# Attention over cached and new keys: the new keys' probabilities turned with the cached ones, their products one step later

## The chip, the cores and the metric

The kernel runs on one core of one Trainium2 chip. The metric is the device time of one execution in microseconds (us), the median over the runs shown. A core has five engines with a queue of instructions each, which they work off in order: TensorE (PE in the profile; PEld is its loading of weights, which overlaps the matmuls), VectorE (DVE), ScalarE (ACT), GpSimd (POOL) and SyncE (SP), which here only issues DMAs. The engines wait for one another by semaphores.

## The reference

`x` is 32 sequences of 32 tokens with 512 features. Four layers each add their result to `x`:

```python
x = x + einsum('bct,bcd->bdt', x, weights[cond])            # a 32x32 mix of tokens, picked per sequence
x = x + x @ W.T + 0.5 * (x @ lora_A[label]) @ lora_B.T      # picked per sequence
x = x + einsum('bsi,boi->bso', x, weight[adapter])          # picked per sequence
x = x + attention(x)
```

The attention has 32 query heads and 8 key heads of 128 features (4 query heads share a key head). Queries and keys are normalised and rotated by position. Each sequence sees 512 cached keys from 16 pages of a paged cache, masked beyond its cached length, and then its own 32 new keys:

```python
scores = einsum('bqhd,bkhd->bhqk', q, k_all) * SCALE        # k_all: 512 cached, 32 new
scores = where(valid, scores, -1e30)
probs = softmax(scores)
o = einsum('bhqk,bkhd->bqhd', probs, v_all)                 # v_all: 512 cached, 32 new
out = einsum('bse,de->bsd', o.reshape(b, s, 4096), Wo)
```

All is fp32.

## The kernel before

The first part (to some 370 us) computes the first three layers and the projections of queries, keys and values; queries, new keys and new values go to DRAM. The change doesn't touch it. The rest, `with tc.manual_schedule(engines=order)` from L1247 on, is the attention. Its order is written out by hand for all five engines: what the loop issues first on an engine runs first there. Waits are put in by the framework, where an instruction needs another's data, buffer or PSUM bank.

The work is cut into units (b, g): sequence b of 32, key head g of 8. A unit has 128 rows: 4 query heads times 32 tokens. One loop step n stands for the unit n = 8 b + g and does, for several units at different stages:

- `scores` (L1012): two matmuls of TensorE give 128x544 scores in `s_ps` (two PSUM banks, one buffer), and one VectorE operation (L1028) scales and masks them into `pr` and takes the row's minimum, `low`. The next step's scores wait until that has read `s_ps`.
- `exponentials` (L1040): ScalarE, in place, with the row's sum in `dens`.
- `flip_kept` (L1144): VectorE transposes finished outputs `os` into `ot`.
- `fill` (to n = 36) or `share`: one piece of another matmul that has no hurry, to fill TensorE: the last of the value projections, later the output projection of an earlier group of four sequences (`finish`, L1174). `SHARE` says how many of its 32 heads each of 32 steps takes, counted from n = 37 (`BEGIN`) on.
- `place` (L1052) for the unit issued four steps before. Four units with g = 0 to 3 or 4 to 7 form a quarter (b, q), and `pr` and `placed` are per quarter, with two buffers each. The products with the values need the probabilities with the keys on the partitions. In its step j of 4 VectorE turns 32x32 blocks of 128x512 elements of the quarter (L1057: `turned`), and four copies of 32x512 move each band of 32 partitions to its place in `placed`: two on ScalarE and two on GpSimd for q = 0, two on ScalarE and two on VectorE for q = 1, with a third on ScalarE in place of one of VectorE's in its last step (sequence 0 has its own split).
- `gather_new`, `flip_new` (L1077, L1082): once a quarter, the probabilities of the new keys, 4 times 32 columns, are gathered by GpSimd into `pq`, turned by TensorE into PSUM (`pn_ps`) and copied by ScalarE into `pn`.
- `values` (L1088) for the unit issued LAG = 8 steps before: four products of `placed` with the cached values, added up in `o_ps`. That is four PSUM banks with one buffer; bank u holds, side by side, the 128 columns of head u of the first quarter and of the second.
- `new_values` (L1110), after the products of g = 3: eight products of `pn` with the new values, four for each quarter.
- `keep` (L1127), after the last products of a quarter: VectorE takes the reciprocal of the sums (`rden`) and scales that quarter's columns of `o_ps` into `os` (L1133).

In each step the loop issues scores, exponentials, `flip_kept`, `fill`, then `gather_new`, `flip_new` and `place`, then `share`, then `values`. Each matmul in the source is two in the profile's counts, for fp32.

Of the kernel before, what the change touches and what calls it, by code (L numbers as in the profile page):

```python
# [12 lines left out]
F32 = mybir.dt.float32  # L13
# [7 lines left out]
P = 128  # L21
B, S, HID = 32, 32, 512
D, HQ, HK = 128, 32, 8
REP = HQ // HK
PAGES, PSIZE, NPP = 64, 32, 16
L = NPP * PSIZE
# [12 lines left out]
QUAD = 4  # L39
AHEAD = 8  # L40
VS_BUFS = 2
LATE = 12
N_LOW = 9


C_BT, C_SEQ, C_TOK, C_LAB, C_COND = 0, 128, 160, 168, 176
# [13 lines left out]
def cond_resid_kernel(  # L60
# [18 lines left out]
    nc = tc.nc  # L79
# [35 lines left out]
    ident = const.tile([P, P], F32, name="ident")  # L115
# [106 lines left out]
    def load_new_keys(b: int):  # L222
        nc.sync.dma_start(out=kts[b][:, NPP, :], in_=k_d[b])
# [672 lines left out]
    tp = turn.enter_context(tc.tile_pool(name="a_t", bufs=1))  # L896
# [99 lines left out]
    ps_p = ctx.enter_context(tc.tile_pool(name="b_p", bufs=1, space=PSUM, side="right"))  # L996
# [5 lines left out]
    tp = ctx.enter_context(tc.tile_pool(name="b_t", bufs=2, side="right"))  # L1002
# [3 lines left out]
    dens, prs, pos = {}, {}, {}  # L1006
    first = L - N_LOW * PSIZE

# [3 lines left out]
    def scores(b: int, g: int):  # L1012
# [5 lines left out]
        q = qt[:, u * REP * S : (u + 1) * REP * S]  # L1018
        nc.tensor.matmul(ps[:, first:L], q, kt4[:, :N_LOW, g, :], start=True, stop=True)  # L1019
        nc.tensor.matmul(  # L1020
            ps[:, L : first + LT], q, kt4[:, N_LOW:, g, :], start=True, stop=True
        )
# [27 lines left out]
    placed = {}  # L1050

    def place(b: int, q: int, j: int):  # L1052
        if j == 0:
            placed[b, q] = tp.tile([P, QUAD, L // P, P], F32, tag="placed", name=f"placed_{b}_{q}")
        pr = prs[b, q][:, :, :L].rearrange("p u (c j s) -> p j u c s", j=P // S, s=S)[:, j]
        part = tp.tile([P, QUAD, L // P, S], F32, tag="turned", name=f"turned_{b}_{q}_{j}")
        nc.vector.transpose(part, pr)  # L1057

        on_pool = q == 0 or b == 0
        if b == 0:  # L1060
            on_act = 1 + q
        else:
            on_act = 3 if q == 1 and j == QUAD - 1 else 2
        for i in range(P // S):
            dst = placed[b, q][j * S : (j + 1) * S, :, :, i * S : (i + 1) * S]
            src = part[i * S : (i + 1) * S]
            dst, src = (a.rearrange("p u c s -> p (u c) s") for a in (dst, src))
            if i < on_act:
                nc.scalar.copy(dst, src)  # L1069
            elif on_pool:  # L1070
                nc.gpsimd.tensor_copy(dst, src)  # L1071
            else:
                nc.vector.tensor_copy(dst, src)  # L1073

    pqs, pns = {}, {}

    def gather_new(b: int, q: int):  # L1077

        pqs[b, q] = tp.tile([P, QUAD, S], F32, tag="pq", name=f"pq_{b}_{q}", bufs=1)
        nc.gpsimd.tensor_copy(pqs[b, q], prs[b, q][:, :, L:])  # L1080

    def flip_new(b: int, q: int):  # L1082
        pnp = ps_p.tile([P, P], F32, tag="p", name=f"pn_ps_{b}_{q}")
        nc.tensor.transpose(pnp, pqs.pop((b, q)).rearrange("p u s -> p (u s)"), ident)  # L1084
        pns[b, q] = tp.tile([P, P], F32, tag="pn", name=f"pn_{b}_{q}")
        nc.scalar.copy(pns[b, q], pnp)

    def values(b: int, g: int):  # L1088

        vt = vts[b]  # L1090
        q, u = divmod(g, QUAD)
        if g == 0:
            pos[b] = ps_o.tile([P, QUAD, L], F32, tag="o", name=f"o_ps_{b}")
        po = pos[b][:, u, q * D : (q + 1) * D]
        pt = placed[b, q][:, u, :, :]
        for c in range(L // P):
            nc.tensor.matmul(  # L1097
                po,
                pt[:, c, :],
                vt[:, c, g * D : (g + 1) * D],  # L1100
                start=(c == 0 and q == 0),
                stop=(c == L // P - 1 and q == 1),
            )
        if u == QUAD - 1:
            if q == 0:
                new_values(b)
            placed.pop((b, q)), prs.pop((b, q))
            keep(b, q)

    def new_values(b: int):  # L1110

        vn = vns[b]
        for q in range(HK // QUAD):
            pn = pns.pop((b, q))
            for i in range(QUAD):
                r = slice(i * S, (i + 1) * S)
                nc.tensor.matmul(  # L1117
                    pos[b][:, i, q * D : (q + 1) * D],
                    pn[r, :],
                    vn[r, q, :],  # L1120
                    start=(q == 1),
                    stop=(q == 0),
                )

    kept = []

    def keep(b: int, q: int):  # L1127

        po = pos[b] if q == 0 else pos.pop(b)
        rden = tp.tile([P, QUAD], F32, tag="rden", name=f"rden_{b}_{q}")  # L1130
        nc.vector.reciprocal(rden, dens.pop((b, q)))  # L1131
        o = tp.tile([P, QUAD * D], F32, tag="os", name=f"os_{b}_{q}")
        nc.vector.tensor_tensor(  # L1133
            o.rearrange("p (u d) -> p u d", d=D),
            po[:, :, q * D : (q + 1) * D],
            rden.unsqueeze(2).to_broadcast([P, QUAD, D]),
            ALU.mult,
        )


        at = BT * HK * (b // BT) + LAG + HK + QUAD - 2 if (b % BT, q) == (0, 1) else 0
        kept.append((b, q, o, at))
# [60 lines left out]
    LAG = 8  # L1203

    SHARE = [1, 1, 2, 1, 1, 1, 1, 1, 2, 1, 1, 1, 1, 1] + [1, 1, 0] + [1] * 7 + [0] + [1] * 7

    LAST = SHARE[:14] + [1, 1, 0, 1, 0, 1, 1, 1, 1, 1, 0, 1, 0] + [1, 1, 1, 2, 2]
    BEGIN = BT * HK + LAG - QUAD + 1  # L1210

    def share(n: int):
        t, i = divmod(n - BEGIN, BT * HK)
        if 0 <= t < NT - 1:
            parts = LAST if t == NT - 2 else SHARE
            done = sum(parts[:i])
# [4 lines left out]
    units = [(b, g) for b in range(B) for g in range(HK)]  # L1221
# [25 lines left out]
    with tc.manual_schedule(engines=order):  # L1247
        for n in range(N + LAG):
            b, g = divmod(n, HK)
            if n == FILLED + 2:  # L1250
                pa.close()
                late = ctx.enter_context(tc.tile_pool(name="b_w", bufs=1))
                places.append(late)
                wos[1] = late.tile([P, LATE, HID], F32, name="wo_1")
            if BEGIN <= n <= N and n % (BT * HK) == 0:

                load_residual((n - BEGIN) // (BT * HK))
            if n < N:
                if g == 0 and b >= 1:
                    load_queries(b, 1)  # L1260
                if g == 0 and 1 <= b < B - 1:
                    load_keys(b + 1)
                    load_new_keys(b + 1)
                    keys.dsts = page_keys(b + 1)
                    keys.transfer(slice(0, 12))
                if g < L // P and b >= 2:
                    load_value_chunk(b, g)
                if g == QUAD and b < B - 1:
                    load_queries(b + 1, 0)
                    load_inverses(b + 1)  # L1270
                    if b >= 1:
                        keys.transfer(slice(12, NPP))
                    if 1 <= b < B - 2:
                        load_table(b + 2)
                if g == QUAD + 1 and b >= 1:
                    load_new_values(b)
                if g == QUAD + 2 and b < B - 2:
                    keys = Picked(nc.sync, k_cache, pages_of.pop(b + 2), range(NPP), K_SHAPE)
                scored = scores(b, g)
                exponentials(*scored)  # L1280
            flip_kept(n)
            fill(n)
            if n in unstored:
                store_values(*unstored.pop(n))
            if n == QUAD + 1:
                load_new_values(0)
            if n in WO_AT:
                load_wo(2 * WO_AT.index(n))
            if QUAD <= n < N + QUAD:
                bq, i = divmod(n - QUAD, HK)  # L1290
                q, j = divmod(i, QUAD)
                if j == 0:
                    gather_new(bq, q)
                if j == 2:
                    flip_new(bq, q)
                place(bq, q, j)
            share(n)
            if n >= LAG:
                values(*units[n - LAG])
            if n < N and g == HK - 1 and b < B - 1:  # L1300
                see_keys(b + 1)
            if n > N + QUAD:
                at = 4 * (n - N - QUAD - 1)
                finish(NT - 1, range(at, at + 4))
        assert not dens and not prs and not pos and not placed and not pns
        load_residual(NT - 1)
        flip_kept(N + LAG)
        finish(NT - 1, range(3 * QUAD, HALF))
        finish_by_halves(NT - 1)
# [76 lines left out]
```

## Time and profile before

| | |
|---|---|
| median of 3 runs (lowest to highest) | 1139.23 us (1138.83 to 1139.81) |
| the profiled execution | 1139.8 us, its span 1138.0 us |
| granted TensorE clock | 1.00 |
| busy: TensorE, VectorE, ScalarE, GpSimd | 99%, 71%, 66%, 49% of the span |
| turns of the new keys' probabilities, TensorE (L1084) | 64, 273 ns each, 17.4 us busy |
| their copies out of PSUM, ScalarE (L1086) | 64, 245 ns each |
| their gathers, GpSimd (L1080) | 64, 290 ns each |
| turns of the others, VectorE (L1057) | 256, 698 ns each |
| copies into `placed`: ScalarE, GpSimd, VectorE | 539 of 617 ns, 268 of 611 ns, 217 of 436 ns |
| scaling into `os`, VectorE (L1133) | 64, 692 ns each |

How to read it: matmuls are pipelined, and their ends are modelled, so a matmul's duration isn't the time by which it holds up the next one; the distance of their starts is. "Idle before" is the time an engine stood still ahead of an instruction, with what released it. A group's line gives its source line, engine, operation, the tiles out<-in, its shape and how often it occurs. In a timeline, like instructions that follow each other are merged into one line (x8: eight of them). The first steps of attention start at 373 us, the last scores at 1089.5 us.

### The profile page before, as it was taken

Reading aid. Unit: us, or ns where it says so; the run is one execution under the profiler, and the core shown is the slowest. Engines: PE = TensorE matmul, PEld = TensorE weight load, DVE = VectorE, ACT = ScalarE, POOL = GpSimd, SP = SyncE. Lnnn points to the kernel's source line nnn. Section 1 sums busy time; section 2 is a strip of 40 time slices with the busy share of each in tenths; the row PEclk is TensorE's granted clock in tenths of the full one; section 3 lists DMA queues with packets and bytes.
Section 4 is the critical chain, followed back from the end, with each engine's and each line's share of the span. In section 5 each row is a group of like instructions: output and inputs, shape, how many; then the busy total and the mean of one; then the engine's idle time right before and its main releaser. Section 6 shows DMA issues by size and latency. Waiting matters only on the chain. (4 is left out here: it accounts for less than half of the span.)

```text
span 1138.0 us, 18994 instructions
## 1 busy us (share of the span) xinstructions
PE 1122.4 (99%) x5432; PEld 730.1 (64%) x5432; DVE 807.5 (71%) x1670; ACT 752.8 (66%) x1900; POOL 559.0 (49%) x719
## 2 busy tenths in 40 slices
PE   8999999999999999999999999999999999999998
PEld 5554444444444577777777777777777777777766
DVE  2510688886977487777778868877877777877851
ACT  1211377576666688777777777877777877777750
POOL 3411689899897544533443344334533443344310
PEclk9999999999999999999999999999999999999999
DMA  8998447688786587888667756765776676766610
GB/s 319 392 419 347 176 133 220 174 234 229 197 232 169 159 272 267 271 308 284 216 217 243 248 190 230 262 229 178 243 251 223 200 239 224 240 202 214 222 29 10
DMA packets 173354, 259.24 MB, mean 228 GB/s; under 512 B 31522, under 2 KB 130466, under 8 KB 168770
## 3 DMA queue, kind: packets, MB, share of 16 engines
q1 hardware_dynamic: 152226, 184.22, 51.0%
q0 software_dynamic: 20016, 71.97, 17.7%
q10 hardware_dynamic: 1008, 1.84, 0.4%
q8 instruction: 44, 0.72, 0.3%
q14 instruction: 60, 0.49, 0.1%
HBM read 228.46 MB, written 37.88 MB: 234 GB/s over the span
## 5 line engine op out<-in xcount | busy, mean ns | idle before, releaser
L1069 ACT COPY placed<-turned 32x512 f32<-32x512 f32 x539 | 332.8, 617 | 31.4 <-DVE turned L1057 24.0
L1097 PEld LDWEIGHTS o_ps<-vt,placed 128*128 128x128 f32 x2048 | 267.0, 191 | 118.5 <-issue 89.4
L1028 DVE CUSTOM_DVE_ANT_0 pr<-s_ps,mask,rq 128x544 f32<-128x544 f32 x256 | 200.6, 784 | 132.5 <-PE s_ps L1020 124.0
L1044 ACT ACTIVATE pr<-pr,low 128x544 f32<-128x544 f32 x256 | 192.2, 751 | 132.7 <-DVE low L1028 130.8
L1071 POOL COPY placed<-turned 32x512 f32<-32x512 f32 x268 | 163.6, 611 | 230.8 <-DVE turned L1057 164.1
L1097 PE MATMUL o_ps<-vt,placed 128*128 128x128 f32 x2048 | 270.4, 275 | 5.6 <-ACT placed L1069 2.8
L1174 PE MATMUL f_ps<-wo,ot 128*128 128x512 f32 x480 | 241.3, 594 | 0.7
L1057 DVE STREAM_TRANSPOSE turned<-pr 128x512 f32<-128x512 f32 x256 | 178.7, 698 | 0.1
L1019 PE MATMUL s_ps<-kt,qt 128*128 128x288 f32 x512 | 174.4, 422 | 1.4 <-DVE low L1028 0.5
L1020 PE MATMUL s_ps<-kt,qt 128*128 128x256 f32 x512 | 152.3, 379 | 0.4 <-issue 0.4
L252 POOL DMA_INDIRECT vt<-in_v_cache_dram,v_idx x128 | 128.0, 1000 | 36.6 <-issue 25.4
L1020 PEld LDWEIGHTS s_ps<-kt,qt 128*128 128x128 f32 x512 | 97.2, 190 | 27.5 <-DMA kt<-in_k_cache_dram 0.8
L434 POOL TENSOR_TENSOR ra<-ra,rs 128x512 f32<-128x512 f32 x80 | 103.9, 1306 | 10.6 <-DVE rs L429 6.4
L1174 PEld LDWEIGHTS f_ps<-wo,ot 128*128 128x128 f32 x480 | 85.8, 190 | 28.6 <-issue 13.9
L1073 DVE COPY placed<-turned 32x512 f32<-32x512 f32 x217 | 94.6, 436 | 5.5
L1080 POOL COPY pq<-pr 128x128 f32<-128x128 f32 x64 | 18.6, 290 | 149.4 <-PE o_ps L1097 94.6
L447 ACT ACTIVATE sq<-x 128x128 f32<-128x128 f32 x256 | 76.4, 302 | 19.3 <-DVE x L405 13.9
L1019 PEld LDWEIGHTS s_ps<-kt,qt 128*128 128x128 f32 x512 | 77.3, 191 | 17.0 <-DVE low L1028 10.6
L544 ACT COPY r<-m 128x512 f32<-128x512 f32 x80 | 46.4, 580 | 52.4 <-PE m L389 51.4
L389 PE MATMUL m<-t_pair,x_sums 128*128 128x512 f32 x160 | 75.3, 593 | 0.6 <-ACT r L544 0.6
L389 PE MATMUL m<-w_pair,x3t 128*128 128x512 f32 x160 | 75.2, 592 | 0.0
L389 PE MATMUL m<-w_pair,x_sums 128*128 128x512 f32 x160 | 72.1, 592 | 0.0
(129 smaller groups left out, 1223.6 us busy)
## 6 DMA issues: line engine op xcount, KB each, us to landing
kt<-in_k_cache_dram SPq DMA_DIRECT2D x512, 128.0 KB
wa<-in_w_adapt_dram SPq DMA_DIRECT2D x32, 1024.0 KB
q_d<-st SPq DMA_DIRECT2D x128, 128.0 KB
qt<-q_d SPq DMA_DIRECT2D x64, 256.0 KB
w_pair<-in_w_qkv_dram SPq DMA_DIRECT2D x20, 512.0 KB
o_d<-in_w_o_dram SPq DMA_DIRECT2D x16, 512.0 KB
wo<-o_d SPq DMA_DIRECT2D x16, 512.0 KB
k_d<-st SPq DMA_DIRECT2D x32, 128.0 KB
```

The costliest lines, as they stand in the source:

```text
L252: nc.gpsimd.indirect_dma_start(out=vts[b][:, c, :], out_offset=None, in_=v_cache, in_offset=bass.IndirectOffsetOnAxis(ap=v_idx[:, at : at ...
L389: nc.tensor.matmul(ps, of[:, k], by[:, k], start=(not more and k == 0), stop=(k == KH - 1), skip_group_check=more,)
L434: nc.gpsimd.tensor_tensor(u.a, u.a, u.s, ALU.add)
L1019: nc.tensor.matmul(ps[:, first:L], q, kt4[:, :N_LOW, g, :], start=True, stop=True)
L1020: nc.tensor.matmul(ps[:, L : first + LT], q, kt4[:, N_LOW:, g, :], start=True, stop=True)
L1028: nc.vector.tensor_tensor_reduce(pr, ps[:, first : first + LT], mask, rqs[b][:, g // QUAD, u : u + 1], 3.0e38, ALU.add, ALU.min, low,)
L1044: nc.scalar.activation(pr, pr, AF.Exp, bias=low, scale=-1.0, accum_out=dens[quad][:, u : u + 1])
L1057: nc.vector.transpose(part, pr)
L1069: nc.scalar.copy(dst, src)
L1071: nc.gpsimd.tensor_copy(dst, src)
L1097: nc.tensor.matmul(po, pt[:, c, :], vt[:, c, g * D : (g + 1) * D], start=(c == 0 and q == 0), stop=(c == L // P - 1 and q == 1),)
L1174: nc.tensor.matmul(pfs[t][:, :HID], ots[t, h // HALF][:, h % HALF, :], wo(h), start=(h == 0), stop=(h == (HQ if t < NT - 1 else HALF) - 1),)
```

## The change

The probabilities of the new keys are no longer gathered, turned by TensorE and copied. `placed` becomes 17 blocks of 128 columns a quarter instead of 4 x 4. In step j of `place` VectorE turns a further 128x32 elements, the new keys' columns of the quarter's unit j, into a 17th block of `turned`; the four copies then move 32x544 elements instead of 32x512, so after step 3 the 17th block holds what `pn` held. `gather_new`, `flip_new` and their tiles go. `new_values` reads the 17th blocks of both quarters. The second quarter's is complete only after its last `place`, so `new_values` moves from the end of `values` of g = 3 to just before `values` of g = 4, one step later; `keep(b, 0)` moves with it. The first output head of each group of four sequences is projected one step later (`SHARE` begins 0, 2, 2 instead of 1, 1, 2).

```diff
+NEW = QUAD * (L // P)
...
     def place(b: int, q: int, j: int):
         if j == 0:
-            placed[b, q] = tp.tile([P, QUAD, L // P, P], F32, tag="placed", name=f"placed_{b}_{q}")
+            placed[b, q] = tp.tile([P, NEW + 1, P], F32, tag="placed", name=f"placed_{b}_{q}")
         pr = prs[b, q][:, :, :L].rearrange("p u (c j s) -> p j u c s", j=P // S, s=S)[:, j]
-        part = tp.tile([P, QUAD, L // P, S], F32, tag="turned", name=f"turned_{b}_{q}_{j}")
-        nc.vector.transpose(part, pr)
+        part = tp.tile([P, NEW + 1, S], F32, tag="turned", name=f"turned_{b}_{q}_{j}")
+        nc.vector.transpose(part[:, :NEW].rearrange("p (u c) s -> p u c s", u=QUAD), pr)
+        nc.vector.transpose(part[:, NEW], prs[b, q][:, j, L:])
...
-            dst = placed[b, q][j * S : (j + 1) * S, :, :, i * S : (i + 1) * S]
+            dst = placed[b, q][j * S : (j + 1) * S, :, i * S : (i + 1) * S]
             src = part[i * S : (i + 1) * S]
-            dst, src = (a.rearrange("p u c s -> p (u c) s") for a in (dst, src))
...
-    def gather_new(b: int, q: int):
-
-        pqs[b, q] = tp.tile([P, QUAD, S], F32, tag="pq", name=f"pq_{b}_{q}", bufs=1)
-        nc.gpsimd.tensor_copy(pqs[b, q], prs[b, q][:, :, L:])
-
-    def flip_new(b: int, q: int):
-        pnp = ps_p.tile([P, P], F32, tag="p", name=f"pn_ps_{b}_{q}")
-        nc.tensor.transpose(pnp, pqs.pop((b, q)).rearrange("p u s -> p (u s)"), ident)
-        pns[b, q] = tp.tile([P, P], F32, tag="pn", name=f"pn_{b}_{q}")
-        nc.scalar.copy(pns[b, q], pnp)
...
-        pt = placed[b, q][:, u, :, :]
+        pt = placed[b, q][:, u * (L // P) : (u + 1) * (L // P), :]
...
-        if u == QUAD - 1:
-            if q == 0:
-                new_values(b)
+        if g == HK - 1:
             placed.pop((b, q)), prs.pop((b, q))
             keep(b, q)
...
-            pn = pns.pop((b, q))
+            pn = placed[b, q][:, NEW, :]
...
+        placed.pop((b, 0)), prs.pop((b, 0))
+        keep(b, 0)
...
-    SHARE = [1, 1, 2, 1, 1, 1, 1, 1, 2, 1, 1, 1, 1, 1] + [1, 1, 0] + [1] * 7 + [0] + [1] * 7
+    SHARE = [0, 2, 2, 1, 1, 1, 1, 1, 2, 1, 1, 1, 1, 1] + [1, 1, 0] + [1] * 7 + [0] + [1] * 7
...
-                if j == 0:
-                    gather_new(bq, q)
-                if j == 2:
-                    flip_new(bq, q)
                 place(bq, q, j)
             share(n)
             if n >= LAG:
+                if units[n - LAG][1] == QUAD:
+                    new_values(units[n - LAG][0])
                 values(*units[n - LAG])
```

More of the change, by code (lines that the diff above doesn't have):

```diff
@@ L1073, in place @@
                 nc.vector.tensor_copy(dst, src)
-    pqs, pns = {}, {}
-    def gather_new(b: int, q: int):
-        pqs[b, q] = tp.tile([P, QUAD, S], F32, tag="pq", name=f"pq_{b}_{q}", bufs=1)
-        nc.gpsimd.tensor_copy(pqs[b, q], prs[b, q][:, :, L:])
-    def flip_new(b: int, q: int):
-        pnp = ps_p.tile([P, P], F32, tag="p", name=f"pn_ps_{b}_{q}")
-        nc.tensor.transpose(pnp, pqs.pop((b, q)).rearrange("p u s -> p (u s)"), ident)
-        pns[b, q] = tp.tile([P, P], F32, tag="pn", name=f"pn_{b}_{q}")
-        nc.scalar.copy(pns[b, q], pnp)
     def values(b: int, g: int):
@@ L1304, in cond_resid_kernel @@
                 finish(NT - 1, range(at, at + 4))
-        assert not dens and not prs and not pos and not placed and not pns
+        assert not dens and not prs and not pos and not placed
         load_residual(NT - 1)
```

## The prediction

> **What bounds the kernel now.** I read the page first, then the waits of the whole run, then the timelines of single engines over one batch, because the answer lies in the order of a few instructions. The profiled execution took 1139.8 us (span 1138.0 us and 1.8 us around it), 0.6 us over the median of the runs shown, 1139.23 us. The engine shares, and the two longest waits of TensorE's weight loads on ScalarE and VectorE in the attention stage:
>
> ```profile
> PE 1122.4 (99%) x5432; PEld 730.1 (64%) x5432; DVE 807.5 (71%) x1670; ACT 752.8 (66%) x1900; POOL 559.0 (49%) x719
> ...
> PEld o_ps L1097 <- ACT placed L1069: 11.0, 30, 1.4
> PEld s_ps L1019 <- DVE low L1028: 10.6, 27, 1.4
> ```
>
> TensorE has work all the time. So what is taken from its queue is gained, and what it is made to wait for is lost in full; the other engines count only where TensorE waits for them. The chain that ended last shows the price of a turn that goes away (start, us, what):
>
> ```profile
> 1087.33 0.43 PE s_ps L1020 x2
> 1087.76 0.11 PE pn_ps L1084
> 1087.87 0.86 PE f_ps L1174 x2
> ```
>
> A matmul's own duration (273 ns for this turn) isn't its price: the next one starts 0.11 us later. Now one common batch around the place that changes; TensorE, with the row that follows on VectorE and ScalarE (start, us; idle before it):
>
> ```profile
> 716.33 1.05 PE L1097 MATMUL o_ps<-vt,placed 128*128 128x128 f32 x8
> 717.31 0.73 PE L1117 MATMUL o_ps<-vn,pn 32*128 32x128 f32 x16
> 717.97 0.75 PE L1019 MATMUL s_ps<-kt,qt 128*128 128x288 f32 x2
> 718.56 0.59 PE L1020 MATMUL s_ps<-kt,qt 128*128 128x256 f32 x2
> 718.99 1.02 PE L1174 MATMUL f_ps<-wo,ot 128*128 128x512 f32 x2
> 719.85 1.05 PE L1097 MATMUL o_ps<-vt,placed 128*128 128x128 f32 x8
> 720.74 0.65 PE L1019 MATMUL s_ps<-kt,qt 128*128 128x288 f32 x2
> ```
> ```profile
> 715.67 0.78 DVE L1028 CUSTOM_DVE_ANT_0 pr<-s_ps,mask,rq 128x544 f32<-128x544 f32 x1 [0.22 <-PE s_ps L1020]
> 716.38 0.71 DVE L1057 STREAM_TRANSPOSE turned<-pr 128x512 f32<-128x512 f32 x1
> 717.12 0.42 DVE L1073 COPY placed<-turned 32x512 f32<-32x512 f32 x1
> 717.56 0.18 DVE L1131 RECIPROCAL rden<-den 128x4 f32<-128x4 f32 x1
> 718.10 0.69 DVE L1133 TENSOR_TENSOR os<-o_ps,rden 128x512 f32<-128x512 f32 x1 [0.37 <-PE o_ps L1117]
> 719.30 0.78 DVE L1028 CUSTOM_DVE_ANT_0 pr<-s_ps,mask,rq 128x544 f32<-128x544 f32 x1 [0.50 <-PE s_ps L1020]
> ```
> ```profile
> 717.37 1.88 ACT L1069 COPY placed<-turned 32x512 f32<-32x512 f32 x3
> ```
> ```profile
> L1097 PEldq EVENT_SEMAPHORE  x1: 51/51/51, 718.8 to 718.8; - x1
> ```
>
> The reader should see three things. The scaling into `os` (718.10 to 718.79) runs under the scores and the output projection (717.97 to 719.85), so TensorE doesn't notice it. In front of the products of g = 4 stands a semaphore instruction (718.8), beside the wait that the weight load itself carries. In the instruction list of the kernel before it waits for `os` of the same batch: `os` is read out of all four banks of `o_ps` and g = 4 writes into the first of them, other columns. And ScalarE's third copy ends at 719.25, just ahead of the weight load at 719.42.
>
> **The change, part by part.** A step is n; I count steps from the batch's first scores, so the products of g = 0 are at +8.
>
> Removed: 64 turns on TensorE, 64 x 0.11 = 7.0 us, all on the path. 64 ScalarE copies of 245 ns and 64 GpSimd gathers of 290 ns lie off it. No DMA is added, removed or moved, and SP's and GpSimd's gathers of values keep their places.
>
> Added on VectorE: 256 turns of 128x32. No row shows one. Proportion from 128x512 (698 ns) gives 44 ns, the smallest reciprocals with a fixed cost (128x4 156 ns, 128x16 205 ns) up to 205 ns. Tensor-tensor rows of 128x512 (692 ns) and 128x256 (396 ns) differ by 1.15 ns a column, which leaves 146 ns for 32 columns; consecutive operations overlap by some 0.08 us (the turn at 1091.29 lasts 0.71 and the reciprocal starts 0.63 after it). I take 0.13 us, between. Copies grow by 1/16: ScalarE 617 ns by some 27 (its 128x256 and 128x512 copies, 376 and 580 ns, differ by 0.8 ns a column), GpSimd 611 by 27 (290 ns at 128 columns), VectorE 420 by some 15.
>
> [...] No run here shows the small turn yet.
>
> Moved: `new_values` with `keep(b, 0)`, from +11 to +12, behind scores and projection, right in front of g = 4. TensorE's own order loses nothing by it. But the wait for `os` at g = 4 now follows at once on the products that `os` needs. In the same common batch: g = 3 starts at 716.33; scores follow 0.89 later (as at 719.85 to 720.74), 717.22; VectorE's reduction starts 1.12 after the scores (714.55 to 715.67), 718.34. From a reduction to `os` with the same operations between, and no wait, the end of the run shows 1.58 us:
>
> ```profile
> 1090.58 0.78 DVE L1028 CUSTOM_DVE_ANT_0 pr<-s_ps,mask,rq 128x544 f32<-128x544 f32 x1 [1.36 <-PE s_ps L1020]
> ...
> 1091.29 0.71 DVE L1057 STREAM_TRANSPOSE turned<-pr 128x512 f32<-128x512 f32 x1
> 1091.92 0.14 DVE L1131 RECIPROCAL rden<-den 128x4 f32<-128x4 f32 x1
> 1092.16 0.69 DVE L1133 TENSOR_TENSOR os<-o_ps,rden 128x512 f32<-128x512 f32 x1
> ```
>
> With 0.13 for the small turn `os` runs from 720.05 to 720.74. TensorE resumes some 0.17 later (0.06 from a release to its weight load, as 697.63 to 697.69, and 0.11 for a first matmul whose weights weren't loaded early): 720.91 against 719.85, +1.06 us. Queued behind that wait on TensorE are the scores of +13, and all else behind them.
>
> VectorE has no pause from +8 to +11, so 0.16 us a step (turn and two copies) piles up there. Scores at +10 wait for it already (its result at 711.61, the weight load at 711.67): +0.16. The reduction at +11 comes 0.26 later, as its 0.22 of idle goes; ScalarE's three copies end at 719.58, the second half of `new_values` at 720.08, and `os` starts at 720.20: a further +0.15. With the turn's 0.11 of step +10 already gone from that, the common batch loses 1.32 us. In one batch of four the transposition of `os` falls in step +10 (the batch before this one, 684 to 698 us): there nothing absorbs the 0.48, ScalarE's copies end at 698.19 instead of 697.63, and g = 4 moves from 697.83 to 699.68; 1.96 with the turn's 0.11. Mean 1.48 us.
>
> Sum: 27 batches x 1.48 = 40.0. Batches 0 to 3, where three of four have no projection to fill the step: 1.9, 1.5, 1.4, 1.5 and 0.7 of lag, 7.0. Batch 31, with no scores beside it, 0.8 (0.13 + 0.69 + 0.17, less some overlap). Seven steps with a projection share of 0 instead of 1, in which the next scores wait some 0.25 for the reduction: 1.7. GpSimd's two longer copies ahead of g = 0 (weight load 707.71, matmul 708.02, little room): 31 x 0.05 = 1.5. Less 7.0. That is +44.0: 1183.8 against the profiled 1139.8, 1183 against the median.
>
> The refill of `placed` costs nothing: its first copy at +12 now waits for `new_values`, but is ready only behind that step's turn (about 720), when the first half of `new_values` is over (719.4). Without that cover it would delay ScalarE by up to 0.6 us a batch, which the stall hides.
>
> [...]
>
> **The rivals.**
> 1. Faster: the g = 4 products aren't held for `os`, since they touch other columns, and ScalarE's third copy is in time, as it has lost 0.49 us of copies a batch. Then 7.0 goes and 1.7 comes: 1134. Against it the semaphore at 718.8. It decides if TensorE loses under 0.22 us a batch (7.0/32). If only the hold is missing and the copies are late, 0.5 x 32 + 6 + 1.7 - 7 gives 1156.
> 2. Only the bare round trip: VectorE isn't late, and `os` starts 0.13 after `new_values`: (0.13 + 0.69 + 0.17 - 0.1) x 32 - 7 + 2 = +23, 1162. For it: VectorE idled 0.50 us ahead of the reduction at 719.30. Against it, that reduction and the turn stand ahead of `os` in VectorE's queue.
> 3. VectorE's backlog reaches ScalarE's copies in every batch as in the one of four: 32 x 1.96 - 7 + 3 = +59, 1198. For it: VectorE's rows touch each other from 707.87 to 715.45. Against it: the 0.22 of idle at 715.67.
>
> **How the numbers follow.** Forecast, 1170 to 1193: 0.63. Rival 2 with its neighbours, 1158 to 1170: 0.13. Rival 3, over 1193: 0.13. Rival 1: 0.05 at some 1156, 0.05 faster, 0.01 no change (0.2%, some 2.3 us, is what a measurement of this kernel can tell). The small turn's ends, 44 and 205 ns, move the sum by -8 and +7. The range 1160 to 1199 leaves out some 0.17. Slower 0.94, same 0.01, faster 0.05.
>
> **What would show it.** Right: in each batch an idle TensorE of 0.8 us or more ahead of the first product of g = 4, released by VectorE's `os`; 32 such waits, 25 to 45 us in all; `pn_ps` gone; small turns of 0.1 to 0.2 us; scores waiting for `low` a little more. Wrong: g = 4 following `new_values` without a pause (rival 1), or the main loss lying in scores that wait for VectorE.

## The result and the profile after

The changed kernel takes 1230.31 us (1229.86 to 1231.39, 6 runs) against 1139.74 us beside it: 1.0798 times as long, 95% interval 1.0784 to 1.0812, or 91 us more. The forecast was 1183 us, slower by 44, with a range of 1160 to 1199. The direction was right, and half of the loss was missing.

The page's line of engine shares of the changed kernel:

```profile
PE 1155.9 (94%) x5368; PEld 739.1 (60%) x5368; DVE 889.6 (72%) x1926; ACT 752.4 (61%) x1836; POOL 541.7 (44%) x655
```

TensorE now stands still for 6% of the span, against 1% before. Who it waits for, first for its matmuls and then for its weight loads (us in total, times, longest us):

```profile
PE o_ps L1085 <- DVE os L1121: 27.9, 32, 1.4
PE s_ps L1020 <- DVE low L1029: 21.4, 34, 0.9
PE o_ps L1103 <- ACT placed L1070: 6.3, 30, 1.0
```
```profile
PEld s_ps L1020 <- DVE low L1029: 54.4, 124, 1.4
PEld o_ps L1085 <- DVE os L1121: 34.0, 32, 1.6
```

The hold of g = 4 behind `os` is there, once in each of 32 batches. But next to it stands a second wait that was small before (10.6 us, 27 times): scores that wait for VectorE's `low`. The groups of VectorE's copies and small turns, from the answers on these lines of the changed kernel (duration in ns: least, median, most), say why:

```profile
L1074 DVE COPY placed<-turned x217: 706/710/717, 418.1 to 1190.4; 32x544 f32<-32x544 f32 x109
L1059 DVE STREAM_TRANSPOSE turned<-pr x256: 166/170/173, 385.7 to 1190.2; 128x32 f32<-128x32 f32 x128
```

A copy of 32x512 took 420 ns. With 6% more columns it takes 710. One batch around the changed place, TensorE and then VectorE:

```profile
734.97 0.75 PE L1020 MATMUL s_ps<-kt,qt 128*128 128x288 f32 x2 [0.68 <-DVE low L1029]
735.56 0.59 PE L1021 MATMUL s_ps<-kt,qt 128*128 128x256 f32 x2
736.00 1.02 PE L1162 MATMUL f_ps<-wo,ot 128*128 128x512 f32 x2
736.95 0.72 PE L1103 MATMUL o_ps<-vn,placed 32*128 32x128 f32 x14
737.82 0.48 PE L1103 MATMUL o_ps<-vn,placed 32*128 32x128 f32 x2 [0.15 <-ACT placed L1070]
739.09 0.38 PE L1085 MATMUL o_ps<-vt,placed 128*128 128x128 f32 x1 [0.78 <-DVE os L1121]
```
```profile
735.67 0.72 DVE L1074 COPY placed<-turned 32x544 f32<-32x544 f32 x1
736.42 0.78 DVE L1029 CUSTOM_DVE_ANT_0 pr<-s_ps,mask,rq 128x544 f32<-128x544 f32 x1
...
737.13 0.71 DVE L1058 STREAM_TRANSPOSE turned<-pr 128x512 f32<-128x512 f32 x1
737.76 0.17 DVE L1059 STREAM_TRANSPOSE turned<-pr 128x32 f32<-128x32 f32 x1
737.85 0.14 DVE L1119 RECIPROCAL rden<-den 128x4 f32<-128x4 f32 x1
738.34 0.69 DVE L1121 TENSOR_TENSOR os<-o_ps,rden 128x512 f32<-128x512 f32 x1 [0.35 <-PE o_ps L1103]
```

Three lateness marks stand in a row: the scores come 0.68 us late behind `low`, the last new products 0.15 us late behind ScalarE's third copy, and g = 4 0.78 us late behind `os`. This is one of the batches, one in four, in which VectorE also transposes finished outputs (L1142) in the step before. In a common batch these scores start 1.13 us after g = 3, here 1.73; the other two marks are the same.

From the starts of the scores' first matmuls one can read how long each step of a batch is. The table has the mean over the steps of the scores of batches 4 to 30, in us, worked out from the timelines of TensorE; column g is the step whose products are those of g (of the batch before, as the products come eight steps behind the scores). The new products (0.66 us) lie in g = 3 before and in g = 4 after. The rows e1 to f1 are experiments told below.

| | 0 | 1 | 2 | 3 | 4 | 5 | 6 | 7 | sum |
|---|---|---|---|---|---|---|---|---|---|
| before | 2.70 | 2.70 | 2.80 | 3.42 | 2.77 | 2.64 | 2.83 | 2.88 | 22.75 |
| after | 2.67 | 3.31 | 3.01 | 3.17 | 5.19 | 2.37 | 2.97 | 2.86 | 25.55 |
| e1, padding | 2.67 | 2.87 | 2.78 | 2.77 | 4.91 | 2.37 | 2.97 | 2.87 | 24.19 |
| e2, products in two | 2.68 | 3.32 | 3.01 | 3.38 | 4.05 | 2.37 | 2.96 | 2.86 | 24.64 |
| e3, both | 2.68 | 2.86 | 2.77 | 3.22 | 3.55 | 2.55 | 2.72 | 2.87 | 23.22 |
| g2, the move alone | 2.67 | 2.71 | 2.81 | 2.72 | 4.77 | 2.43 | 3.07 | 2.86 | 24.04 |
| f1, new products behind g = 3 and 7 | 2.75 | 2.71 | 2.69 | 3.20 | 2.93 | 2.62 | 2.72 | 3.39 | 23.01 |

Per batch the change costs 2.80 us: 1.23 in g = 1 to 3 (0.61, 0.21 and, without the moved products, 0.41), 1.76 in g = 4 (again without them), less 0.18 in the rest. Over 27 batches that is 75.6 us; batches 0 to 3 give 9.9, the last one 2.7, start and tail 2.2. These sum to the 90.4 us by which the span grew.

### The profile page after: what moved, and what is told of

Same layout as the page of the kernel before. It is cut to its first block, busy times and chain, and to the rows that moved or that the text cites. A ratio compares the mean times of both kernels' runs of the same rounds, so it can differ in the third digit from the quotient of the medians.

```text
span 1228.4 us, 19001 instructions
## 1 busy us (share of the span) xinstructions
PE 1155.9 (94%) x5368; PEld 739.1 (60%) x5368; DVE 889.6 (72%) x1926; ACT 752.4 (61%) x1836; POOL 541.7 (44%) x655
## 5 line engine op out<-in xcount | busy, mean ns | idle before, releaser
L1072 POOL COPY placed<-turned 32x544 f32<-32x544 f32 x268 | 169.9, 634 | 481.8 <-DVE rden L1119 246.9
L1070 ACT COPY placed<-turned 32x544 f32<-32x544 f32 x539 | 345.8, 642 | 37.2 <-DVE turned L1059 31.3
L1085 PE MATMUL o_ps<-vt,placed 128*128 128x128 f32 x2048 | 273.6, 277 | 31.8 <-DVE os L1121 27.9
L1020 PE MATMUL s_ps<-kt,qt 128*128 128x288 f32 x512 | 181.1, 435 | 26.1 <-DVE low L1029 21.4
L1074 DVE COPY placed<-turned 32x544 f32<-32x544 f32 x217 | 154.3, 711 | 5.5
L253 POOL DMA_INDIRECT vt<-in_v_cache_dram,v_idx x128 | 123.3, 964 | 39.8 <-issue 29.6
L435 POOL TENSOR_TENSOR ra<-ra,rs 128x512 f32<-128x512 f32 x80 | 103.8, 1303 | 10.6 <-DVE rs L430 6.3
L1162 PEld LDWEIGHTS f_ps<-wo,ot 128*128 128x128 f32 x480 | 90.6, 190 | 27.3 <-issue 17.2
L500 DVE STREAM_TRANSPOSE st<-ra 128x512 f32<-128x512 f32 x80 | 56.3, 704 | 15.8 <-DMA q_d<-st 5.5
```

What stands on the lines that cost most here:

```text
L253: nc.gpsimd.indirect_dma_start(out=vts[b][:, c, :], out_offset=None, in_=v_cache, in_offset=bass.IndirectOffsetOnAxis(ap=v_idx[:, at : at ...
L1085: nc.tensor.matmul(po, pt[:, c, :], vt[:, c, g * D : (g + 1) * D], start=(c == 0 and q == 0), stop=(c == L // P - 1 and q == 1),)
L1162: nc.tensor.matmul(pfs[t][:, :HID], ots[t, h // HALF][:, h % HALF, :], wo(h), start=(h == 0), stop=(h == (HQ if t < NT - 1 else HALF) - 1),)
```

## The experiments

The kernel before ran beside each of them; it took 1139.74 to 1142.64 us on different chips, so only the ratios are compared. A hundredth is 11.4 us.

### e1: the copies' source in blocks, like their destination

```diff
-        part = tp.tile([P, NEW + 1, S], F32, tag="turned", name=f"turned_{b}_{q}_{j}")
+        part = tp.tile([P, NEW + 1, S + 1], F32, tag="turned", name=f"turned_{b}_{q}_{j}")[:, :, :S]
```

> The changed kernel with one word of padding behind each block of `turned`, so that the copies' source is 17 blocks of 32 like their destination, and not 544 columns in one piece. Theory: VectorE's copies of 32x544 take 710 ns instead of 420 because source and destination no longer split alike into halves (544 against 17 blocks); with 17 on both sides they fall to some 440 ns, steps g = 1 to 3 lose some 0.3 us a batch instead of 1.2, and the time to some 1185 us (1170 to 1195), since the hold at g = 4 stays. Rival: 17 blocks are odd or 544 columns too many in themselves; then the copies stay at 710 ns and the time at 1230.

Measured: 1.0415 (1.0397 to 1.0432), 47 us over the kernel before, as the theory had it. The copies, of the same 32x544 elements, in the list of costliest groups of this kernel:

```profile
L1074 DVE COPY placed<-turned 32x544 f32<-32x544 f32 x217 | 97.8, 451 | 5.5
```

451 ns instead of 711 on average. So neither the 17 blocks nor the 544 columns are slow in themselves. Step g = 1 falls from 3.31 to 2.87, and TensorE's own wait for `low` from 21.4 to 3.4 us; the hold stays (28.6 us). 44 us of the 91 hang on this one property of 217 copies.

### g1: how many blocks

```diff
-                nc.vector.tensor_copy(dst, src)
+                k = 15 - j % 2
+                nc.vector.tensor_copy(dst[:, :k], src[:, :k])
+                nc.vector.tensor_copy(dst[:, k:], src[:, k:])
```

> The kernel before, each of VectorE's copies of 16 blocks cut in two: 15 and 1 blocks in the even steps of a quarter, 14 and 2 in the odd ones. It measures single copies, not the time. [...] Rival (544 columns are too many): 32x480 takes 400 to 410 ns.

It was run once, for the rows, in the kernel before (shape, count, busy us, mean ns):

```profile
L1074 DVE COPY placed<-turned 32x480 f32<-32x480 f32 x124 | 79.9, 644 | 3.0
L1074 DVE COPY placed<-turned 32x448 f32<-32x448 f32 x93 | 36.6, 394 | 2.6
L1075 DVE COPY placed<-turned 32x64 f32<-32x64 f32 x93 | 20.7, 223 | 0.0
L1075 DVE COPY placed<-turned 32x32 f32<-32x32 f32 x124 | 20.7, 167 | 0.0
```

480 columns cost 644 ns, 512 cost 420; the rival's 400 to 410 ns didn't come. The 15 blocks are slow, 14 and 16 are fast (394 and 420 ns). In the changed kernel the 17 blocks take 711 ns from a source in one piece; with the padding it is 17 blocks on both sides, and 451 ns. What makes 15 and 17 blocks slow against a source in one piece no run shows.

### e4: slow copies alone

```diff
-                nc.vector.tensor_copy(dst, src)
+                nc.vector.tensor_tensor(dst, src, src, ALU.max)
```

VectorE's 217 copies into `placed` become a maximum of the source with itself, which gives the same values; nothing else differs from the kernel before. It stands for the longer copies of the changed kernel: 711 ns on average there against 436, some 0.27 us a copy.

> [...] Theory: VectorE has no slack from the second quarter's first step on, so most of the 0.27 us a copy reaches TensorE through late scores: 7 copies a batch, 0.9 to 1.2 us a batch, 1168 to 1180. Rival: VectorE's 29% of idle covers it: 1139 to 1148.

Measured: 1.0241 (1.0223 to 1.0258), 27 us, with copies of 683 ns on average (436 in the kernel before). The theory's range held. Without any other part of the change, VectorE's 217 longer copies (54 us more busy time) cost TensorE half of that, although VectorE is idle for 29% of the span in the kernel before. Most of what idle time is left lies in the steps g = 5 to 7: 3.5 of 4.2 us a batch in this run, worked out from its timeline, and some 0.1 us in each of g = 1 to 4. In the changed kernel slow copies cost more, the 44 us of e1; what makes the difference no run shows.

### e2: the first quarter's products stay where they were

```diff
+            if q == 0:
+                new_values(b, 0)
...
-                    new_values(units[n - LAG][0])
+                    new_values(units[n - LAG][0], 1)
```

> The changed kernel with new_values cut in two: the first quarter's four products and keep(b, 0) go back to the end of g = 3, the second quarter's stay ahead of g = 4. VectorE's operations are the same. Theory: the hold of g = 4 behind os is a cost of its own, some 0.9 to 1.2 us a batch of 32, so the time falls to some 1195 (1187 to 1203) and no idle of TensorE ahead of g = 4 is put down to os. Rival: VectorE's backlog is the bound and the hold only shows where it is waited for; then TensorE waits elsewhere and the time stays above 1215.

Measured: 1.0505 (1.0488 to 1.0523), 58 us over the kernel before and 33 below the changed one, within the theory's range. Step g = 4 falls from 5.19 to 4.05 (half of the new products moved back to g = 3), g = 1 and 2 stay. TensorE's waits in this kernel:

```profile
PE s_ps L1020 <- issue: 12.0, 21, 0.7
PE o_ps L1104 <- DVE os L1120: 10.5, 30, 1.4
PE s_ps L1020 <- DVE low L1029: 6.1, 14, 0.9
```

No product of g = 4 waits for `os` any more. The second quarter's new products ahead of it (L1104) do, for 10.5 us, against my expectation: VectorE is so late with its slow copies that even an `os` issued a step earlier isn't always ready. So the hold is a cost of its own, and a part of it came back as lateness.

### g2: the move alone

```diff
-            if q == 0:
-                new_values(b)
...
+        keep(b, 0)
...
+                if units[n - LAG][1] == QUAD:
+                    new_values(units[n - LAG][0])
```

> The kernel before with the move alone: new_values, still from pn, with keep(b, 0), just ahead of g = 4, and SHARE as in the changed kernel. No turn or copy is changed. Theory: the hold of g = 4 behind os costs by itself what the prediction gave it without the small turn, 0.93 us a batch: 32 x 0.93 and 1.7 for SHARE, some 31 us, 2.3 to 3.2% slower. Rival: without VectorE's backlog the hold is short, the bare way there and back less what it replaces: under 1.5%.

Measured: 1.0358 (1.0342 to 1.0374), 41 us: a hold, and dearer than I had expected. Step g = 4 is longer by 1.34 us without the moved products, the whole batch by 1.29. TensorE in one batch:

```profile
812.99 0.75 PE L1019 MATMUL s_ps<-kt,qt 128*128 128x288 f32 x2
...
814.96 0.73 PE L1116 MATMUL o_ps<-vn,pn 32*128 32x128 f32 x16
816.74 1.13 PE L1097 MATMUL o_ps<-vt,placed 128*128 128x128 f32 x8 [1.05 <-DVE os L1133]
```

and VectorE beside it:

```profile
814.32 0.78 DVE L1028 CUSTOM_DVE_ANT_0 pr<-s_ps,mask,rq 128x544 f32<-128x544 f32 x1 [0.31 <-PE s_ps L1020]
...
815.90 0.69 DVE L1133 TENSOR_TENSOR os<-o_ps,rden 128x512 f32<-128x512 f32 x1
```

From the reduction to `os` it is 1.58 us, as read from the end of the profile of before, and `os` to g = 4 is 0.84, against 0.86 worked out. The first piece is longer than predicted: the reduction starts 1.33 us after these scores, not 1.12, and they themselves start 1.05 after g = 3, not 0.89. But this batch, too, is one of those with the transposition of finished outputs. Over the products of batches 4 to 30, 27 batches, g = 4 starts 4.73 us after g = 3 in the mean, where the prediction's working without the small turn gives 4.45. In 15 common batches it is 4.54; there only the way from the scores to the reduction is longer, 1.23. In six, like the one above, it is 4.80. In the other six it is 5.13, as VectorE adds a finished group's output to `x` between the reduction and `os`, which the prediction's sum doesn't have:

```profile
573.64 0.65 DVE L1183 TENSOR_TENSOR x<-x,f_ps 128x512 f32<-128x512 f32 x1
```

### e3: both edits

> Both edits together, and SHARE as in the kernel before. Theory: the two costs are most of the 91 us and add up; what is left is the small turn, 170 ns 256 times, and ScalarE's longer copies against the 7.0 us of turns saved on TensorE: 1140 to 1155. Rival: a third cost of over 0.7 us a batch that neither theory names; then over 1165.

Measured: 1.0136 (1.0120 to 1.0153), 15.5 us over the kernel before, at the upper end of what the theory gave. e1 takes away 3.83 hundredths, e2 2.93, both with `SHARE` 6.62: the two add up nearly in full. What is left is mostly in g = 4 (3.55 against 2.77 + 0.33) and g = 1 (2.86 against 2.70); the weight loads of the second quarter's new products wait 17.2 us for ScalarE's third copy.

### f1: the second quarter's new products behind g = 7

```diff
-            if q == 0:
-                new_values(b, 0)
+            new_values(b, q)
...
-                if units[n - LAG][1] == QUAD:
-                    new_values(units[n - LAG][0], 1)
```

> Both edits (padding, and the first quarter's new products back at the end of g = 3), and the second quarter's new products moved from ahead of g = 4 to behind g = 7, where nothing they read is recent. Theory: of the 15 us that both edits left over the kernel before, some 0.4 us a batch is TensorE waiting there for ScalarE's third copy; it goes, so 10 to 14 us less than with both edits: within 0.5% of the kernel before, from either side. Rival: g = 4 itself waits for the same copies, and nothing is gained: 1.2 to 1.5% slower than the kernel before.

Measured: 1.0082 (1.0068 to 1.0096), 9.3 us over the kernel before; expected was within 0.5%. 6 us came back, not 10 to 14: g = 4 itself now waits for the third copy (its weight loads for 23.3 us, 11.0 before). So theory and rival both have a part in it.

The rest of f1 is in its row of the table, 0.26 us a batch over before. It isn't idle time: TensorE is busy for 1131.8 us here and for 1122.4 before, and stands still for some 15.7 in both. Taking half of the new products out of g = 3 saves 0.22 there, and putting it behind g = 7 costs 0.51. Eight matmuls of one half take 0.43 us until the next scores start (below), all sixteen in the kernel before took 0.66 (717.31 to 717.97). And each piece starts 0.98 us after the products ahead of it, where scores without new products between start after 0.89:

```profile
732.27 1.05 PE L1085 MATMUL o_ps<-vt,placed 128*128 128x128 f32 x8
733.26 0.50 PE L1103 MATMUL o_ps<-vn,placed 32*128 32x128 f32 x8
733.69 0.75 PE L1020 MATMUL s_ps<-kt,qt 128*128 128x288 f32 x2
```

So cutting the new products in two costs 0.29 us a batch here. With 0.21 more in g = 4 and g = 0, and 0.22 less in g = 2 and g = 6, where the turns were, that is the row. e2 and e3 cut the new products in two as well. A version that keeps them in one piece behind g = 7 was not run.

### e5: the small turn alone

```diff
+        nc.vector.transpose(part[:, 0, 0, :], prs[b, q][:, j, L:])
         nc.vector.transpose(part, pr)
```

> The kernel before with the small turn alone: in each place VectorE turns the new keys' 128x32 into a part of `turned` that the large turn then overwrites; nothing uses it. Theory: 170 ns a turn, some 0.1 us of VectorE's time each, of which only what falls into the steps without slack (g = 0 to 3) reaches TensorE, 0.15 to 0.3 us a batch: +5 to +10 us, 0.4 to 0.9%. Rival: VectorE's idle covers it, within 0.2%.

Measured: 1.0157 (1.0143 to 1.0171), 17.9 us, where 5 to 10 were expected. The experiment is dearer than the thing it stands for: the spare turn takes 206 ns at the median here, not 170, and VectorE is idle for 13.4 us between it and the large turn, whose output it shares. So 17.9 us is likely more than the small turns cost in the changed kernel; how much more isn't shown. Step g = 1 grows most, by 0.31.

### f2 and f3: copies moved to GpSimd

f2 is f1 and this edit, f3 the kernel before and this edit:

```diff
-            on_act = 3 if q == 1 and j == QUAD - 1 else 2
+            on_act = 2
...
-            elif on_pool:
+            elif on_pool or (j == 2 and i == 3) or j == 3:
```

> As the kernel with the new products behind g = 7, and in the second quarter GpSimd takes one copy of step 2 and two of step 3 (from VectorE and ScalarE, which keep two, two, one and none, and two each). Theory: VectorE's steps without slack and ScalarE's third copy are what is left, so this beats the kernel before: 0.3 to 1.0% faster. Rival: GpSimd's copies come later than those they replace, behind its gathers, and g = 4 waits for them: no faster than the kernel with the new products behind g = 7.

> The kernel before with that split of the second quarter's copies alone, as a control. Theory: it takes away the waits for the third copy and the late scores that the kernel before has too, some 0.1 to 0.3 us a batch: 0.2 to 0.8% faster, and less than the kernel that has the new keys' change as well, by up to the 7.0 us of TensorE's turns. Rival: the split alone gains as much or more, and the new keys' change is worth nothing even when repaired.

Measured: 1.2164 (1.2147 to 1.2180) and 1.2205 (1.2179 to 1.2231), both far slower. GpSimd's waits in f2, then in f3:

```profile
POOL placed L1072 <- DMA vt<-in_v_cache_dram,v_idx: 243.6, 46, 7.6
```
```profile
POOL placed L1071 <- DMA vt<-in_v_cache_dram,v_idx: 313.9, 57, 9.5
```

In the instruction list of f3 GpSimd's copies of the second quarter wait until the cached values' gathers that stand ahead of them in its queue have landed, and TensorE waits for the copies (173 us in f2, 181 in f3). The waits in these two lines are 5.3 and 5.5 us each on average. Why the framework puts that wait there I have not found out. Both expectations fell, and nothing follows from this pair on the new keys.

### g3 and g4: the mask on GpSimd

VectorE's mask, which opens its stretch without slack, issued on GpSimd: g3 in the kernel before, g4 in f1.

```diff
+                if g == HK - 1 and b < B - 1:
+                    see_keys(b + 1, nc.gpsimd)
...
-            if n < N and g == HK - 1 and b < B - 1:
-                see_keys(b + 1)
```

> The kernel before with the next sequence's mask (VectorE, 0.64 us a batch, issued last in step g = 7) done by GpSimd right behind that step's exponentials. Theory: VectorE's stretch without slack begins there, so scores at g = 1 and the copies ahead of g = 4 come earlier: 0.2 to 0.6% faster. Rival: GpSimd's two copies of that step come later by the mask, and g = 0 waits for them: no faster.

> The kernel with padding and the new products behind g = 3 and g = 7, and the mask on GpSimd as well. Theory: what is left of it over the kernel before, 0.8%, is VectorE's small turns in the steps without slack; 0.64 us a batch less there takes away half or more: 0.0 to 0.5% slower than the kernel before. Rival: the loss lies in ScalarE's longer copies, and it stays at 0.7 to 0.9%.

Measured: 1.0241 (1.0227 to 1.0255) and 1.0288 (1.0274 to 1.0302). The rival holds in g3: GpSimd takes 2.1 us for what VectorE does in 0.64, its copies come late, and g = 0 waits (step 0: 3.67 instead of 2.70; TensorE's weight loads wait 54.6 us for GpSimd's copies, 14.1 in the kernel before). The line of the mask in g3:

```profile
L218 POOL TENSOR_SCALAR mask<-key_i,len_f 128x544 f32<-128x544 int16 x31 | 65.2, 2104 | 28.0 <-DVE low L1028 27.9
```

g4 fails by the same delay (2102 ns for the mask, 37.5 us of weight loads that wait for GpSimd's copies, 5.4 in f1), so it doesn't tell the small turns from ScalarE's longer copies. No version that was run beats the kernel before.

## Why the prediction was wrong

**Where the bound lies.** Right: TensorE's queue, with the other engines counting only where it waits for them.

**Turns removed, 7.0 us.** No run measured it alone. The turns are gone (5432 matmuls to 5368) and their 0.11 us shows as g = 6 falls from 2.83 to 2.72 in e3, which has the `SHARE` of before.

**The longer copies.** This is the step that failed. ScalarE's 27 ns and GpSimd's 27 ns are 25 and 23 in the profile. For VectorE "some 15" ns were taken from the share of added columns; it was 275 (436 to 711). With that, VectorE's backlog isn't 0.16 us a step but about 0.7 (an estimate from 2 x 0.275 and the turn) in the first three steps of the second quarter. The prediction had itself said that VectorE has no pause there, so it had the place and the lever, but the wrong weight on it. e1 takes the wrong term away: 1.0415 times 1139.74 is 1187 us, against the forecast of 1183. That it comes so close is partly luck, as two other errors nearly cancel. Per batch, the hold costs 1.29 (g2) where the sum had 0.93. Small turn, backlog and ScalarE's copies then add 0.37 (e1's 1.44 and the 0.22 of the turns, less 1.29) where the sum had 0.55 (1.48 less 0.93).

**The small turn.** 0.13 us taken between ends of 0.04 and 0.20; 0.17 long, 0.10 from its start to that of the next VectorE operation, 0.20 to that of a copy. Right in size. (The difference of the tensor-tensor rows leaves 137 ns for 32 columns, not 146; the 0.13 doesn't hang on it.)

**The hold of g = 4.** Right in mechanism and in count: 32 waits for `os`, 27.9 us idle, where 25 to 45 us in waits of 0.8 or more were named (most are 0.78). Its price was low: the move alone costs 1.29 us a batch in a kernel without the small turn, for which the prediction's working gives 0.93. 0.28 of the difference lies between g = 3 and g = 4: 0.13 in the way from the scores to the reduction, which was read from the step before, 0.13 in VectorE's addition to `x` in some batches, which was left out, and the rest in scores that come late in some.

**The backlog and ScalarE's copies.** Right in kind: g = 1 is the step that suffers most after g = 4, and the prediction had named the scores that end it as waiting for `low` already. ScalarE's third copy holds the new products in 30 of 32 batches.

**The refill of `placed`.** No wait of ScalarE for the new products is among those listed, as said; GpSimd waits for them once, 9.4 us, and TensorE's weight loads wait for GpSimd's copies 15.8 us in all, little more than the 14.1 before.

**The rivals.** Rival 3, VectorE's backlog in every batch, is the case that came, for a reason that was not in it; its 1198 was bounded by a copy that costs next to nothing. Rival 1 and 2 didn't come. Of the signs of being wrong, the main loss in scores that wait for VectorE came by less than half: 1.23 of 2.80 us a batch lie in g = 1 to 3. The range counted the small turn's ends but none for the copies, because a row of nearly the same shape seemed to be a price and not a guess.

After both repairs no version that was run is worth it: the best, f1, is still 0.8% slower. It saves 0.22 us of TensorE a batch with the turns, pays 0.29 for new products in two pieces and 0.21 in g = 4 and g = 0. How these 0.21 divide among the small turns, ScalarE's longer copies and the two pieces stays open, and so does whether the new products in one piece behind g = 7 would pay.

## What to carry to other kernels

A row for nearly the same shape isn't the price of the new shape. When an edit makes a block count odd, or makes source and destination of a VectorE copy divide differently, run that one copy first; here 15 and 17 blocks against a source in one piece took 644 and 711 ns where 14 and 16 took 394 and 420, and padding the source by one word per block gave 260 of 275 ns back. When a short run of small matmuls is cut in two, each half can cost more than half: 0.51 us for the one that was moved, 0.22 saved where it had been. When a reader of an accumulator is moved, ask what writes to the same PSUM banks right behind it: a scaling that cost nothing under other work became 1.3 us a batch of TensorE's time when nothing was left between it and the next products. Idle time of an engine in the mean (29% of VectorE here) says nothing about the steps in which it has none.

## What the runs showed of the hardware

- A VectorE copy of 32x480 fp32 took 644 ns and one of 32x512 took 420 ns, for 15 and 16 blocks of a strided destination and a source in one piece.
- GpSimd's comparison of 128x544 took 2104 ns; the same operation on VectorE took 640 on average, between 464 and 857.
- TensorE's granted clock was 1.00 in the kernel before and 0.926 over the run of f2; there it was 0.88 in the stretch from 400 to 500 us, in which TensorE was busy for 77 us of 100. The eight matmuls of a unit's products that start there at 434.50 us, after TensorE had stood still for 8.01 us, took 2.07 us, and those that start at 423.89 us 1.05.
